# Causal row maxima of an attention block: the diagonal's 128 keys masked in SBUF instead of by products into PSUM

## The chip, the core and the metric

The kernel runs on one core of a Trainium2 chip. The metric is device time in microseconds (us). Three runs of the kernel before took 963.00, 969.34 and 960.15 us; their median is 963.0 us.

## What is computed

One transformer block over 8 sequences of 512 tokens with 256 channels: causal attention with 16 heads of 16 channels, plus a gated memory term, then a layer norm, then a mixture of 8 true experts, then a layer norm. Cut to what matters here:

```
scores = einsum('bhtd,bhsd->bhts', q, k) * scale        # per batch and head, 512 x 512
scores = where(causal, -inf, scores)
attn   = softmax(scores, axis=-1)                       # needs the maximum of each row t over s <= t
seq    = einsum('bhts,bhsd->bhtd', attn, v)
x      = layernorm(x + (seq + gated * mem_val) @ out_w.T + out_b)
expert = einsum('td,edh->teh', x, expert_w) + expert_b  # all 8 experts for every token
x      = layernorm(x + einsum('te,teh->th', combine_w, expert))
```

All data is float32.

## The kernel before

**Units and half steps.** Attention is worked off in 32 units, a unit being one batch b and a group g of four heads (`UNITS`, line 148). The main loop (lines 788 to 818) runs over units u, then over i = 0 to 3, then over pr = 0, 1. One pass of the innermost loop is called a half step here; there are eight to a unit. Two units are in work at once in each half step, in `products(u, i, pr)` (line 174):

- for unit m = u + 1, the products q k for the row maxima: `mx`, with 128 query tokens (block t) on the partitions and the n = 128, 512, 384 or 256 keys of the causal row (for i = 0, 1, 2, 3) along the free axis, for two heads (line 184). `mx` is a tile of two PSUM banks, one for each head, and there is one such tile (`psA`, bufs=1);
- for unit u (or u - 1 when i is 0), the products k q that become the softmax: `sc` (line 188), also one tile of two banks. ScalarE takes their exponential into `pe` (line 197), and GpSimd zeroes the masked part of its first 128 columns (line 199).

The two heads of `mx` and the two of `sc` use different groups of 32 rows of TensorE[...].

**The mask of the maxima.** After the products, line 191 adds a mask to the last 128 columns of each head's `mx`: a bfloat16 identity times a bfloat16 tile that holds -1e30 above the diagonal, accumulated in PSUM. Then VectorE takes the negated maximum over all n columns (line 194) into `negmax`, one column for each head and block. When all 16 columns of a unit are there, `turn_largest(u)` (line 203), called in half step (u, 0, 0), turns them by a TensorE transpose into `pt` (line 206), ScalarE copies the result (line 208), and a DMA on ScalarE's queue puts it as one more channel into the q tile of the unit (line 209), so that `sc` comes out with the maximum already taken off. The `sc` products of that unit begin in half step (u, 1, 0).

**Other fixed work of a half step.** In set half steps come `project_qk` (line 157, with two ScalarE evictions, line 161), `project_v` (line 167, one ScalarE copy, line 169), and, when pr is 1, `values` (line 220), the product of `pe` and v.

**The order of the work.** Instructions run on each engine in the order in which the Python code issues them (`in_this_order`, line 57). What fills a half step behind its fixed work is chosen by a planner at build time, `fill(need)` (line 755). It adds `need` (from `TAKE`, less `PQ`, `PV`, `PO`) and an allowance to a credit, capped at 3.0; the allowance is `EARLY` = 0.6 until the first batch's router is done (`ready`), and `MORE` = 0.9 from then on. It then lets chains of generators (`front`, `lines`, `memory_...`) and, while the credit is over 0.4, the bulk (`memory_sums`, `all_experts`) issue their next piece, and takes off what each `yield` says that it costs. `front(b)` (line 597) is the output projection, first norm and router of a batch, which must wait for that batch's attention (`done`). `all_experts(b)` (line 691) is its 16 expert pieces, of four matmul records each (line 707), each with two VectorE operations (line 711), and its second norm. `front` may be at most two batches ahead of the finished experts (line 624) and loads its input at most four ahead (line 552). After the attention, a loop (line 821) issues all that is left; it is called the tail here.

**Other engines' work that the steps touch.** GpSimd multiplies the attention output by the softmax denominators (`osb`, line 577) and prepares the residual (lines 560 to 566). VectorE evicts the output projection (lines 611 and 613) and the experts.

Of the kernel before, what the change touches and what calls it, by code (L numbers as in the profile page):

```python
# [9 lines left out]

F32 = mybir.dt.float32
BF16 = mybir.dt.bfloat16
AF = mybir.ActivationFunctionType
ALU = mybir.AluOpType
AX = mybir.AxisListType

P = 128
B, T, D, H, DH = 8, 512, 256, 16, 16
NT = T // P
KC = D // P  # L20
NG = 4
NE, NTRUE = 10, 8
MASKED = -1.0e30
# [1 line left out]


TAKE = (0.85, 1.6, 1.35, 1.1)
EARLY, MORE = 0.6, 0.9
PV, PQ, PO = 1.2, 2.15, (1.05, 0.85, 0.65, 0.45)
ROUNDS = (2, 1, 1, 1)  # L30
AHEAD = 5
# [36 lines left out]
def block_kernel(ctx, tc, x, xT, wqk, bqk, wtok, wod, memv, memvb, row, gw, we, eb, out):  # L68
    nc = tc.nc
    PS = bass.MemoryType.PSUM  # L70
    const = ctx.enter_context(tc.tile_pool(name="const", bufs=1))
# [3 lines left out]
    att = ctx.enter_context(tc.tile_pool(name="att", bufs=2))  # L75
# [28 lines left out]

    ws = const.tile([P, KC, NTRUE, D], F32, name="ws")
    nc.sync.dma_start(ws[:, :, 0, :], memv.rearrange("(k p) c -> p k c", p=P))
    ebs = const.tile([NTRUE, D], F32, name="ebs")
    wo = const.tile([P, KC, D], F32, name="wo")
    nc.sync.dma_start(wo, wod.rearrange("(k p) o -> p k o", p=P))
    mb = const.tile([P, KC, 2], F32, name="mb")  # L110
# [3 lines left out]
    for b in range(1, B):  # L114
# [3 lines left out]

    ident = const.tile([P, P], F32, name="ident")
    make_identity(nc, ident)  # L120
    identb = const.tile([P, P], BF16, name="identb")
    nc.vector.tensor_copy(identb, ident)

    mask_ts = const.tile([P, P], BF16, name="mask_ts")
    nc.gpsimd.memset(mask_ts, 0.0)
    nc.gpsimd.affine_select(out=mask_ts, in_=mask_ts, compare_op=ALU.is_ge, fill=MASKED,
                            base=0, pattern=[[-1, P]], channel_multiplier=1)
    half = const.tile([P, NT], F32, name="half")
    nc.gpsimd.memset(half, -0.5)
    first = const.tile([P, NE], F32, name="first")  # L130
# [18 lines left out]
    qk = {}  # L149
# [24 lines left out]
    def products(u, i, pr):  # L174
        m, t = u + 1, (0, 3, 2, 1)[i]
        v, j = (u, i - 1) if i else (u - 1, NT - 1)
        n = T - j * P
        mx = m < len(UNITS) and psA.tile([P, 2, T], F32, tag="mx", name=f"mx{m}_{t}_{pr}")
        sc = 0 <= v < len(UNITS) and psA.tile([P, 2, T], F32, tag="sc", name=f"sc{v}_{j}_{1 - pr}")
        for h in range(2):  # L180
            if mx:

                r = slice(32 * (2 * pr + h), 32 * (2 * pr + h) + 32)
                nc.tensor.matmul(mx[:, h, :n], qk[m, 0][r, n - P : n], qk[m, 1][r, :n], start=True, stop=False)  # L184
            if sc:

                r = slice(32 * (2 - 2 * pr + h), 32 * (2 - 2 * pr + h) + 32)
                nc.tensor.matmul(sc[:, h, :n], qk[v, 1][r, j * P : (j + 1) * P], qk[v, 0][r, j * P :], start=True, stop=True)  # L188
        if mx:
            for h in range(2):  # L190
                nc.tensor.matmul(mx[:, h, n - P : n], identb, mask_ts, start=False, stop=True)  # L191
            if m not in negmax:
                negmax[m] = att.tile([P, 4, NT], F32, name=f"negmax{m}", tag="negmax")
            nc.vector.tensor_reduce(negmax[m][:, 2 * pr : 2 * pr + 2, t], mx[:, :, :n], AX.X, ALU.max, negate=True)  # L194
        if sc:
            pe = att.tile([P, 2, T], F32, tag="pe", name=f"pe{v}_{j}_{1 - pr}", bufs=4)
            nc.scalar.activation(pe[:, :, :n], sc[:, :, :n], AF.Exp, scale=DH**-0.5)  # L197

            nc.gpsimd.affine_select(out=pe[:, :, :P], in_=pe[:, :, :P], compare_op=ALU.is_ge, fill=0.0,  # L199
                                    base=0, pattern=[[0, 2], [1, P]], channel_multiplier=-1)  # L200
            pes[j, 1 - pr] = pe

    def turn_largest(u):

        pt = bank(f"pt{u}")
        nc.tensor.transpose(pt[:H, :P], negmax.pop(u).rearrange("p j i -> p (j i)"), ident)
        nt = att.tile([H, P], F32, name=f"nt{u}", tag="nt")
        nc.scalar.copy(nt, pt[:H, :P])
        nc.scalar.dma_start(qk[u, 0][0 if u % 2 else DH :: 32], nt)

    negmax = {}
    pes, pos = {}, {}

    def values(u, j):
# [39 lines left out]
    def fold_values():  # L254

        wd, mv = wo, ws[:, :, 0, :]
        for c in range(KC):
            pw = bank(f"pw{c}")
            for k in range(KC):
                nc.tensor.matmul(pw[:, :D], mv[:, k, c * P : (c + 1) * P], wd[:, k, :],  # L260
                                 start=(k == 0), stop=(k == KC - 1))
            nc.scalar.copy(wt[:, c, CM : CM + D], pw[:, :D])
            yield 0.9
        for n in range(2):
            mbb = ws[:, :, 1 + n, :P]
            nc.vector.tensor_copy(mbb, bc(mb[:, :, n], 2, P))
            pw = bank(f"pwb{n}")
            for k in range(KC):
                nc.tensor.matmul(pw[:, :D], mbb[:, k, :], wd[:, k, :], start=(k == 0), stop=(k == KC - 1))
            if n == 0:  # L270
                nc.scalar.copy(b2, pw[:, :D])
            else:
                nc.vector.tensor_tensor(ob2, pw[:, :D], vec("ob"), ALU.add)
            yield 0.9
        for k in range(KC):
            nc.sync.dma_start(ws[:, k], we[:, k * P : (k + 1) * P, :].rearrange("e p h -> p e h"))
        nc.sync.dma_start(ebs, eb)

    memp = ctx.enter_context(tc.tile_pool(name="mem", bufs=1))
    turned, lined, gates = set(), set(), set()  # L280
# [268 lines left out]
    ffp = []  # L549

    def prepare(b):
        yield lambda: lines_over and b < left[0] + 4
        if not ffp:
            ffp.append(ctx.enter_context(tc.tile_pool(name="ff", bufs=2)))
        ff = ffp[0]

        xb = st[b]["xb"] = ff.tile([P, NT, D], F32, tag="x1", name=f"x1_{b}", bufs=4)
        nc.sync.dma_start(xb, x[b].rearrange("(c p) d -> p c d", p=P))
        yield POOL
        nc.gpsimd.tensor_tensor(xb, xb, bc(ob2, 1, NT), ALU.add)  # L560
        yield lambda: b // HALF in gates
        for c in range(0, NT, 2):
            yield POOL
            gb2 = ff.tile([P, 2, D], F32, tag="recs", name=f"gb2_{b}_{c}")
            nc.gpsimd.tensor_tensor(gb2, bc(b2, 1, 2), bc(gated[:, c : c + 2, b], 2, D), ALU.mult)
            nc.gpsimd.tensor_tensor(xb[:, c : c + 2], xb[:, c : c + 2], gb2, ALU.add)
        yield lambda: b in done
        recs = []
        for k in range(KC):
            recs.append(ff.tile([P, T], F32, name=f"recs{b}_{k}", tag="recs"))  # L570
            nc.sync.dma_start(recs[k], bc(st[b]["dr"][k], 1, DH))
        yield STEP
        yield STEP
        yield POOL
        for k in range(KC):
            o = st[b]["osb"][:, k, :]
            nc.gpsimd.tensor_tensor(o, o, recs[k], ALU.mult)
        yield STEP
# [112 lines left out]
    def all_experts(b):  # L691

        yield lambda: b in ready
        ff = ffp[0]
        x1, x1T, cw = (st[b][n] for n in ("x1", "x1T", "cw"))
        pc = bank(f"pc{b}")
        for c in range(NT):
            nc.tensor.matmul(pc[:NTRUE, c * P : (c + 1) * P], cw[:, c, :], ident, start=True, stop=True)
        cT = ff.tile([NTRUE, T], F32, tag="cT", name=f"cT_{b}", bufs=1)
        nc.scalar.copy(cT, pc[:NTRUE, :])  # L700
        yield 0.8
        mv2 = ff.tile([P, NT, 2], F32, tag="mv", name=f"mv2_{b}")
        for c in range(NT):
            for ep in range(NTRUE // 2):
                pe = bank(f"pex{b}_{c}_{ep}")
                for k in range(KC):
                    nc.tensor.matmul(pe, x1T[:, k, c * P : (c + 1) * P],  # L707
                                     ws[:, k, 2 * ep : 2 * ep + 2, :].rearrange("p e h -> p (e h)"),
                                     start=(k == 0), stop=(k == KC - 1))
                for e in range(2):  # L710
                    nc.vector.scalar_tensor_tensor(x1[:, c, :], pe[:, e * D : (e + 1) * D],  # L711
                                                   cw[:, c, 2 * ep + e : 2 * ep + e + 1], x1[:, c, :], ALU.mult, ALU.add)
                yield 1.75
            pb = bank(f"pbias{b}_{c}")
            nc.tensor.matmul(pb[:, :D], cT[:, c * P : (c + 1) * P], ebs, start=True, stop=True)  # L715
            nc.vector.tensor_tensor(x1[:, c, :], x1[:, c, :], pb[:, :D], ALU.add)
            stats(mv2, x1, c, f"b{b}")
            yield 0.45
        rr = root(mv2, f"b{b}")
        yield STEP  # L720
        for c in range(NT):
            norm(x1, x1, mv2, rr, c)
            nc.sync.dma_start(out[b, c * P : (c + 1) * P, :], x1[:, c, :])
        left[0] += 1
# [158 lines left out]
```

## Time and profile before

| | |
|---|---|
| median of three runs | 963.0 us |
| the profiled execution: its time, its span | 966.05 us, 964.2 us |
| TensorE (PE) busy, its weight loads | 885.6 us (92%), 426.0 us |
| VectorE (DVE) | 606.8 us (63%) |
| ScalarE (ACT) | 309.6 us (32%) |
| GpSimd (POOL) | 313.3 us (32%) |
| mean granted TensorE clock | 0.962 |

The span is the time from the first to the last instruction of the profiled execution; 1.85 us of its time lie around it. In the rows of operations, `L194 DVE ... x256 | 209.4, 818` means line 194, VectorE, 256 instructions, 209.4 us in total and 818 ns each in the mean. TensorE's records overlap and their ends are modelled, so the distance between the starts of two groups says more than their durations. A float32 matmul leaves two records.

### The profile page before, as it was taken

Reading aid. Unit: us, or ns where it says so; the run is one execution under the profiler, and the core shown is the slowest. Engines: PE = TensorE matmul, PEld = TensorE weight load, DVE = VectorE, ACT = ScalarE, POOL = GpSimd, SP = SyncE. Lnnn points to the kernel's source line nnn. Section 1 sums busy time; section 2 is a strip of 40 time slices with the busy share of each in tenths; the row PEclk is TensorE's granted clock in tenths of the full one; section 3 lists DMA queues with packets and bytes.
Section 4 is the critical chain, followed back from the end, with each engine's and each line's share of the span. In section 5 each row is a group of like instructions: output and inputs, shape, how many; then the busy total and the mean of one; then the engine's idle time right before and its main releaser. Section 6 shows DMA issues by size and latency. Waiting matters only on the chain.

```text
span 964.2 us, 14019 instructions
## 1 busy us (share of the span) xinstructions
PE 885.6 (92%) x5360; PEld 426.0 (44%) x5360; DVE 606.8 (63%) x1293; ACT 309.6 (32%) x606; POOL 313.3 (32%) x501
## 2 busy tenths in 40 slices
PE   6999987888788899999999999999999999979996
PEld 3544443444354454354544344543444344334442
DVE  1234657886966656756766866556655676577765
ACT  4164633344324233333323333332333332200000
POOL 1067763536363422521153113211231124230000
PEclk9799988999889799999999999999999999999998
DMA  7300000000000000100100000000000010020000
GB/s 247 95 11 16 11 7 4 3 2 24 4 23 24 13 14 10 39 2 3 39 30 1 2 26 23 23 1 22 28 23 1 4 46 23 3 67 1 22 22 22
DMA packets 25459, 23.67 MB, mean 25 GB/s; under 512 B 8324, under 2 KB 21132, under 8 KB 25392
## 3 DMA queue, kind: packets, MB, share of 16 engines
q1 hardware_dynamic: 24288, 22.22, 7.2%
q8 instruction: 42, 0.69, 0.3%
q10 hardware_dynamic: 1056, 0.40, 0.2%
q0 software_dynamic: 48, 0.16, 0.1%
q14 instruction: 25, 0.20, 0.1%
HBM read 16.73 MB, written 4.73 MB: 22 GB/s over the span
## 4 chain that ended last, share of the span: by engine, by line
PE 69%; DVE 16%; POOL 6%; DMA 3%; issue 3%; ACT 2%; SPq 0%; POOLq 0%; DVEq 0%; ACTq 0%
PE pex L707 22%; PE mx L184 14%; PE po L220 5%; PE pq L157 5%; DVE negmax L194 5%; PE mx L191 4%; PE pa L606 3%; PE pa L609 3%; PE pv L167 2%; PE sc L188 2%; DVE x L711 2%; DMA s<-w 2%; PE pbias L715 2%; PE pm L475 1%; DVE pr L485 1%
## 5 line engine op out<-in xcount | busy, mean ns | idle before, releaser
L197 ACT ACTIVATE pe<-sc 128x1024 f32<-128x1024 f32 (+3 forms) x256 | 180.1, 704 | 415.6 <-PE sc L188 400.0
L194 DVE TENSOR_REDUCE negmax<-mx 128x2 f32<-128x256 f32 (+3 forms) x256 | 209.4, 818 | 154.3 <-PE mx L191 153.9
L184 PE MATMUL mx<-qk,qk 32*128 32x128 f32 (+3 forms) x1024 | 226.7, 500 | 48.3 <-DVE negmax L194 45.8
L199 POOL TENSOR_SCALAR_AFFINE_SELECT pe<-pe 128x256 f32<-128x256 f32 x256 | 104.6, 409 | 475.4 <-ACT pe L197 475.0
L707 PE MATMUL pex<-ws,x1T 128*128 128x512 f32 x512 | 242.1, 606 | 3.7 <-DVE dn L683 2.1
L188 PE MATMUL sc<-qk,qk 32*128 32x512 f32 (+3 forms) x1024 | 217.4, 497 | 2.4 <-ACT pe L197 1.2
L711 DVE SCALAR_TENSOR_TENSOR x<-pex,cw,x 128x256 f32<-128x256 f32 x256 | 123.5, 482 | 92.8 <-PE pex L707 86.8
L184 PEld LDWEIGHTS mx<-qk,qk 32*128 32x128 f32 x1024 | 86.5, 190 | 170.6 <-DVE negmax L194 93.1
L707 PEld LDWEIGHTS pex<-ws,x1T 128*128 128x128 f32 x512 | 90.7, 190 | 112.2 <-issue 104.2
L220 PE MATMUL po<-pe,v_aug 128*32 128x512 f32 (+3 forms) x1024 | 98.9, 459 | 0.0
L188 PEld LDWEIGHTS sc<-qk,qk 32*128 32x128 f32 x1024 | 81.8, 189 | 11.5 <-ACT pe L197 4.7
L191 PEld LDWEIGHTS <-identb 128*128 128x128 bf16 x512 | 29.3, 98 | 119.3 <-issue 112.1
L191 PE MATMUL mx<-mask_ts,identb 128*128 128x128 bf16 x512 | 74.9, 229 | 0.0
L157 PE MATMUL pq<-xt,wq 128*128 128x512 f32 x128 | 65.5, 638 | 5.9 <-DMA xt<-in_xT 5.9
L161 ACT ACTIVATE qk<-pq,bq 128x512 f32<-128x512 f32 x64 | 46.3, 773 | 31.6 <-PE pq L157 31.6
L475 PE MATMUL pm<-ou,dm 128*128 128x144 f32 x256 | 48.4, 320 | 1.6 <-DVE pr L485 1.6
L475 PEld LDWEIGHTS pm<-ou,dm 128*128 128x128 f32 x256 | 39.2, 208 | 17.3 <-issue 12.4
L446 POOL TENSOR_TENSOR ou<-jw,jf 128x288 f32<-128x288 f32 x64 | 43.7, 688 | 1.3
L167 PE MATMUL pv<-wt,xt 128*128 128x256 f32 x128 | 37.9, 423 | 0.0
L585 POOL TENSOR_TENSOR rr_b<-rs_b,half 128x4 f32<-128x4 f32 x8 | 8.1, 1006 | 90.3 <-DVE rs_b L583 90.3
L483 DVE SCALAR_TENSOR_TENSOR ou<-pm,last,ou 32x288 f32<-32x288 f32 x48 | 25.2, 525 | 18.8 <-POOL ou L446 12.8
L319 PE MATMUL pl<-wt,xt 128*128 128x272 f32 x128 | 36.6, 423 | 0.0
(162 smaller groups left out, 872.9 us busy)
## 6 DMA issues: line engine op xcount, KB each, us to landing
xt<-in_xT SPq DMA_DIRECT2D x8, 512.0 KB
x<-in_x SPq DMA_DIRECT2D x8, 512.0 KB
recs<-dr SPq DMA_DIRECT2D x16, 256.0 KB
out_y<-x SPq DMA_DIRECT2D x32, 128.0 KB
ws<-in_we SPq DMA_DIRECT2D x2, 1024.0 KB
s<-w SPq DMA_DIRECT2D x8, 127.0 KB
qk<-nt ACTq DMA_DIRECT2D x32, 8.0 KB
wq<-in_wqk SPq DMA_DIRECT2D x3, 128.0 KB
```

The source lines that it names most:

```text
L157: nc.tensor.matmul(pq, wq[:, k, w, g // 2, :], xt[:, b, k, :], start=(k == 0), stop=(k == KC - 1))
L167: nc.tensor.matmul(pv[:, :D], xt[:, b, k, c * P : (c + 1) * P], wt[:, k, CV : CV + D], start=(k == 0), stop=(k == KC - 1))
L184: nc.tensor.matmul(mx[:, h, :n], qk[m, 0][r, n - P : n], qk[m, 1][r, :n], start=True, stop=False)
L188: nc.tensor.matmul(sc[:, h, :n], qk[v, 1][r, j * P : (j + 1) * P], qk[v, 0][r, j * P :], start=True, stop=True)
L191: nc.tensor.matmul(mx[:, h, n - P : n], identb, mask_ts, start=False, stop=True)
L194: nc.vector.tensor_reduce(negmax[m][:, 2 * pr : 2 * pr + 2, t], mx[:, :, :n], AX.X, ALU.max, negate=True)
L197: nc.scalar.activation(pe[:, :, :n], sc[:, :, :n], AF.Exp, scale=DH**-0.5)
L199: nc.gpsimd.affine_select(out=pe[:, :, :P], in_=pe[:, :, :P], compare_op=ALU.is_ge, fill=0.0, base=0, pattern=[[0, 2], [1, P]], channel_mu ...
L220: nc.tensor.matmul(pos[u][32 * h : 32 * h + 32, j * P :], v_aug[b % 2][:, j, 4 * (g // 2) + h, g % 2 : g % 2 + 2].rearrange("p q d -> p (q ...
L475: nc.tensor.matmul(pm[:, i * HALF * 36 : (i + 1) * HALF * 36], dms[h + i], ou[:, i], start=True, stop=True)
L707: nc.tensor.matmul(pe, x1T[:, k, c * P : (c + 1) * P], ws[:, k, 2 * ep : 2 * ep + 2, :].rearrange("p e h -> p (e h)"), start=(k == 0), sto ...
L711: nc.vector.scalar_tensor_tensor(x1[:, c, :], pe[:, e * D : (e + 1) * D], cw[:, c, 2 * ep + e : 2 * ep + e + 1], x1[:, c, :], ALU.mult, AL ...
```

## The change

The two mask products of each half step go, with the bfloat16 constants that fed them. In their place ScalarE copies the last n - 128 to n columns of `mx` (for two heads, 128x256 elements) into an SBUF tile `dia` (two buffers); GpSimd puts the causal mask in there; VectorE takes the maximum of the other n - 128 columns from PSUM at once (not for t = 0, which has none) and the maximum of `dia` in the next half step, after that half step's own reduction. The two results lie in two tiles, and `turn_largest` joins them with an elementwise minimum (they are negated) ahead of the transpose. The planner's allowance `MORE` goes from 0.9 to 1.3. The expert biases `ebs` move from the constant pool to the expert pool, their load to the first `prepare`, and the tile `nt` has one buffer instead of two.

```diff
-EARLY, MORE = 0.6, 0.9
+EARLY, MORE = 0.6, 1.3
...
-    identb = const.tile([P, P], BF16, name="identb")
-    nc.vector.tensor_copy(identb, ident)
-
-    mask_ts = const.tile([P, P], BF16, name="mask_ts")
-    nc.gpsimd.memset(mask_ts, 0.0)
-    nc.gpsimd.affine_select(out=mask_ts, in_=mask_ts, compare_op=ALU.is_ge, fill=MASKED,
-                            base=0, pattern=[[-1, P]], channel_multiplier=1)
...
-                nc.tensor.matmul(mx[:, h, :n], qk[m, 0][r, n - P : n], qk[m, 1][r, :n], start=True, stop=False)
+                nc.tensor.matmul(mx[:, h, :n], qk[m, 0][r, n - P : n], qk[m, 1][r, :n], start=True, stop=True)
...
+        behind = list(diagonal)
+        diagonal.clear()
         if mx:
-            for h in range(2):
-                nc.tensor.matmul(mx[:, h, n - P : n], identb, mask_ts, start=False, stop=True)
             if m not in negmax:
-                negmax[m] = att.tile([P, 4, NT], F32, name=f"negmax{m}", tag="negmax")
-            nc.vector.tensor_reduce(negmax[m][:, 2 * pr : 2 * pr + 2, t], mx[:, :, :n], AX.X, ALU.max, negate=True)
+                negmax[m] = [att.tile([P, 4, NT], F32, name=f"{n_}{m}", tag=n_) for n_ in ("negmax", "negdia")]
+
+            dia = att.tile([P, 2, P], F32, tag="dia", name=f"dia{m}_{t}_{pr}")
+            nc.scalar.copy(dia, mx[:, :, n - P : n])
+            nc.gpsimd.affine_select(out=dia, in_=dia, compare_op=ALU.is_ge, fill=MASKED,
+                                    base=0, pattern=[[0, 2], [-1, P]], channel_multiplier=1)
+            if t:
+                nc.vector.tensor_reduce(negmax[m][0][:, 2 * pr : 2 * pr + 2, t], mx[:, :, : n - P], AX.X, ALU.max, negate=True)
+            diagonal.append((negmax[m][1][:, 2 * pr : 2 * pr + 2, t], dia))
+        for to, dia in behind:
+            nc.vector.tensor_reduce(to, dia, AX.X, ALU.max, negate=True)
         if sc:
...
     def turn_largest(u):
         pt = bank(f"pt{u}")
-        nc.tensor.transpose(pt[:H, :P], negmax.pop(u).rearrange("p j i -> p (j i)"), ident)
-        nt = att.tile([H, P], F32, name=f"nt{u}", tag="nt")
+        most, least = negmax.pop(u)
+        nc.vector.tensor_tensor(least[:, :, 1:], least[:, :, 1:], most[:, :, 1:], ALU.min)
+        nc.tensor.transpose(pt[:H, :P], least.rearrange("p j i -> p (j i)"), ident)
+        nt = att.tile([H, P], F32, name=f"nt{u}", tag="nt", bufs=1)
...
-        nc.sync.dma_start(ebs, eb)
...
+            ffp.append(ffp[0].tile([NTRUE, D], F32, name="ebs", bufs=1))
+            nc.sync.dma_start(ffp[1], eb)
```

More of the change, by code (lines that the diff above doesn't have):

```diff
@@ L11 @@
 F32 = mybir.dt.float32
-BF16 = mybir.dt.bfloat16
 AF = mybir.ActivationFunctionType
@@ L106, in block_kernel @@
     nc.sync.dma_start(ws[:, :, 0, :], memv.rearrange("(k p) c -> p k c", p=P))
-    ebs = const.tile([NTRUE, D], F32, name="ebs")
     wo = const.tile([P, KC, D], F32, name="wo")
@@ L205, in turn_largest @@
         pt = bank(f"pt{u}")
-        nc.tensor.transpose(pt[:H, :P], negmax.pop(u).rearrange("p j i -> p (j i)"), ident)
-        nt = att.tile([H, P], F32, name=f"nt{u}", tag="nt")
+        most, least = negmax.pop(u)
+        nc.vector.tensor_tensor(least[:, :, 1:], least[:, :, 1:], most[:, :, 1:], ALU.min)
+        nc.tensor.transpose(pt[:H, :P], least.rearrange("p j i -> p (j i)"), ident)
+        nt = att.tile([H, P], F32, name=f"nt{u}", tag="nt", bufs=1)
         nc.scalar.copy(nt, pt[:H, :P])
         nc.scalar.dma_start(qk[u, 0][0 if u % 2 else DH :: 32], nt)
-    negmax = {}
+    negmax, diagonal = {}, []
     pes, pos = {}, {}
@@ L714, in all_experts @@
             pb = bank(f"pbias{b}_{c}")
-            nc.tensor.matmul(pb[:, :D], cT[:, c * P : (c + 1) * P], ebs, start=True, stop=True)
+            nc.tensor.matmul(pb[:, :D], cT[:, c * P : (c + 1) * P], ffp[1], start=True, stop=True)
             nc.vector.tensor_tensor(x1[:, c, :], x1[:, c, :], pb[:, :D], ALU.add)
```

## The prediction

> **What bounds the kernel now.** I read the chain that ended last first, then busy time in three stretches: before the first batch's router is done (311), to the end of attention (845), and the tail.
>
> ```profile
> PE 69%; DVE 16%; POOL 6%; DMA 3%; issue 3%; ACT 2%; SPq 0%; POOLq 0%; DVEq 0%; ACTq 0%
> ...
> 0.00:311.00 311.00, 264.51 (x1753) 138.99 (x1753) 182.34 (x332) 130.61 (x304) 149.33 (x252) 0.92 0.12 36
> 311.00:845.00 534.00, 516.36 (x3311) 237.39 (x3311) 342.89 (x748) 174.81 (x294) 150.50 (x239) 0.98 0.06 18
> 845.00:964.20 119.20, 104.72 (x304) 49.65 (x302) 81.57 (x214) 4.17 (x9) 13.46 (x11) 0.98 0.07 24
> ```
>
> After the stretch come its length, then PE, PEld, DVE, ACT and POOL busy. From 311 to 845 TensorE is busy 97% (17.6 us idle) and sets the end; before 311 it idles 46 us, waiting on others; the tail has 14.5 us of idle. So time taken from TensorE's queue counts whole in the middle stretch, about half in the first, and a wait put into that queue counts likewise.
>
> **Removed: the mask products.** What they occupy is seen from starts: mask start to the start of what follows.
>
> ```profile
> 500.86 0.69 PE L184 MATMUL mx<-qk,qk 32*128 32x512 f32 x1
> ...
> 501.93 0.29 PE L191 MATMUL mx<-mask_ts,identb 128*128 128x128 bf16 x2
> ...
> 502.14 0.43 PE L220 MATMUL po<-pe,v_aug 128*32 128x128 f32 x8
> ...
> 822.21 1.13 PE L188 MATMUL sc<-qk,qk 32*128 32x512 f32 x4
> ...
> 823.26 0.43 PE L220 MATMUL po<-pe,v_aug 128*32 128x128 f32 x8
> ```
>
> The products start the mask 1.07 us after themselves, the mask takes 0.21 more; in the last unit, which has no `mx` and no mask, the next work starts after 1.05. So the whole 0.21 goes. Over all half steps it is 0.22 us ahead of `values` (122 of them), 0.125 ahead of most else: 122 x 0.22 + 130 x 0.125 = 43 us. Some 172 half steps lie behind 311 (29 us, whole), 84 before (14 us, half): **-36 us**.
>
> **Added, in parallel.** ScalarE: 256 copies of 128x256 from PSUM; the `v_aug` copy of that shape takes 0.372 us, so +95 us (310 to 405 of 964). GpSimd: 256 selects of 128x256 at 0.409 (L199): +105 us (313 to 418). VectorE: the L194 forms take 1.224, 0.953, 0.679 and 0.417 us, so cutting 256 elements off and reducing them apart costs 0.953 + 0.417 - 1.224 = 0.146, three times of four: +28 us, and 32 minima. None becomes the bound by sum; in the first stretch, where VectorE's work already holds TensorE up, 64 half steps x 0.15 x half = **+5 us**. The ScalarE copy stands ahead of the exponential, which frees `sc`: 0.37 us later, hidden under `values` and the fill (1 to 3 us) that TensorE runs before the next `sc`; `PE sc L188 <- ACT pe L197` is 1.2 us in all. The select of `dia` stands ahead of that of `pe`: 0.41 later, and `values` reads it a half step on. VectorE reads `dia` a half step (3.1 us) after the copy, behind which at most one GpSimd operation of up to 2.4 us stands: hidden; without that cover the evictions of the fill, queued behind it, would be late. The `ebs` move is one 8 KB load, long before its use: nothing. One `nt` buffer: its reader, a DMA, is done a unit (24 us) before: nothing.
>
> **The new order on one bank.** `mx` is freed by VectorE's reduction alone:
>
> ```profile
> L194 DVE TENSOR_REDUCE negmax<-mx 128x2 f32<-128x1024 f32 x64 | 78.3, 1224 | 65.8 <-PE mx L191 65.7
> ...
> L169 ACT COPY v_aug<-pv 128x256 f32<-128x256 f32 x32 | 11.9, 372 | 19.8 <-PE pv L167 18.9 <-PE sc L188 0.6
> ...
> PE mx L184 <- DVE negmax L194: 45.8, 52, 4.2
> ```
>
> By the rows, copy and shortened reduction read different columns and could run together: mx free 0.95 us after the products, 0.4 to 0.5 earlier than by mask and reduction (0.2 + 1.22). The Trainium skill, "PSUM — Partial Sum Buffer", section "PSUM bank collisions raise a hardware error", speaks against that: two engines on one bank and quadrant collide even as two readers at different columns, so they must be ordered. Both instructions touch both banks, so I expect the reduction to wait for the copy: 0.37 + 0.95 + some 0.1 of handing over = 1.42, as before. No run here shows two engines at one bank. By the rows alone some 52 x 0.4 = 20 us of TensorE's 45.8 us of waits would go (sum 957); by the rule nothing. I take the rule: **0**, ends -20 and, where ScalarE is late with evictions of q, k (1.45 us a pair), +25.
>
> **The new wait: the transpose.** Before, `pt` used maxima finished a half step earlier. Now in (u, 0, 0) VectorE must finish the fill of the last half step, reduce the last `dia`, take the minimum; then TensorE transposes, and all of its queue stands behind that. At unit 21:
>
> ```profile
> 564.55 1.98 PE L707 MATMUL pex<-ws,x1T 128*128 128x512 f32 x4
> ...
> 566.58 1.00 DVE L711 SCALAR_TENSOR_TENSOR x<-pex,cw,x 128x256 f32<-128x256 f32 x2 [1.96 <-PE pex L707]
> ...
> 567.03 0.27 PE L206 MATMUL pt<-ident,negmax 128*16 128x128 f32 x1
> ```
>
> VectorE evicts the expert piece until 567.58; then 0.42 (reduction of 256) + 0.2 (small tensor_tensor, L658) + 0.1 = 568.3, while TensorE, without mask, is at `pt` at 566.9: a stall of 1.4 us. The DMA behind `pt` (2.4 us to its use, unit 19) moves with it, as does the work between: nothing more. Behind an output projection VectorE is 1.2 us behind `pt`, and it is 2.0; behind an empty half step 0.15. Worked out so at all 32 transposes of this trace, 34 us. The minimum also reads two SBUF operands: a 40-element operation of that kind (L680, usually 0.2) took 2.22 us beside a GpSimd operation of 2.36:
>
> ```profile
> 853.73 2.36 POOL L560 TENSOR_TENSOR x<-x,ob 128x1024 f32<-128x1024 f32 x1 [11.47 <-DMA x<-in_x]
> ...
> 853.92 2.22 DVE L680 TENSOR_TENSOR w<-w,ex 128x40 f32<-128x40 f32 x1
> ```
>
> The Trainium skill, "SBUF — State Buffer", "Who interferes with whom", gives this as a rule (such an operation and a GpSimd one that reads SBUF exclude each other); by the usual row the minimum costs 0.2, by the rule up to 0.4 more behind a select, 32 x 0.4 = 13 us as an upper end. With `MORE` 1.3 the half step before a transpose holds a piece in 20 of the last 21 units (next part): 20 x 1.35 = 27, and 8 for the earlier ones, where TensorE waits anyway: **+35 us**, ends 12 and 48.
>
> **MORE.** A batch (4 units, 32 half steps) earns: TAKE 4 x 2 x 4.9 = 39.2, less 1.2 (i = 0), 4 x 2.15 (PQ), 4 x 1.2 (PV), 4 x 3.0 (PO), plus 32 x 0.9: 41.4. It asks for 10.8 (front: 4 x 1.9 + 2 x 0.7 + 2 x 0.9) and 30.6 (experts: 0.8 + 16 x 1.75 + 4 x 0.45): 41.4 as well, so the experts stay some three batches behind. At 1.3 it earns 54.2. I followed `fill`'s bookkeeping through the yields for both values; for 0.9 it gives the trace's order (first expert batch done in unit 17, 465 us; second in 21, 571). At 0.9, 82 of 128 pieces are out by the end of attention, at 1.3 112: batches 0 to 6, with batch 7 alone left. A piece costs 1.77 us in the tail; in attention, half steps alike but for it differ by 1.2 (515.64 to 518.00 without, 562.91 to 566.47 with) to 1.8, by least squares over all 1.5; I take 1.6. So attention grows by 30 x 1.6 + 7 (biases, routers) = 55. The tail can't shrink below batch 7's own path from the last `values` (844.8), by the timeline's pieces: denominators out, inverted and back 10; GpSimd's products 3.7; projections and statistics 7.6 (865.7 to 873.3); norm 3; transposes and router products 3.5; expert choice 5.5; experts 4 x 7.69 (909.31 to 917.00 is one of four); end 8.4 (955.8 to 964.2): 73 us. Nothing is left to cover its first 33, where the profile before still had experts of batches 5 and 6. So the tail loses 119 - 74 = 45: **+10 us**, ends -5 (if that path is shorter) and +20 (a piece at 1.9).
>
> **Sum.** 966 - 36 + 5 + 0 + 35 + 10 = 980 us for an execution like the profiled one; the median of the runs lies 3 lower: **977 us**, own range 963 to 992. Chance 0.5.
>
> **Rivals.** (1) *Faster.* The stall at the transpose replaces waits that came later anyway: VectorE catches up while TensorE stands, and the waits on `negmax` (45.8 us) shrink by as much. Then 980 - 35 = 945, about 942 after the 3 us. For it: VectorE is 63% busy; against: from 311 on those waits are only 14.2 us. It decides once less than 0.5 us of each stall is net. Chance 0.18. (2) *ScalarE becomes a link in every half step*: the copy waits behind late evictions, the reduction behind the copy, the next `mx` behind both: 0.1 us x 256 = +25: 1002. For it: 1.45 us evictions in 64 half steps; against: ScalarE is 42% busy after. Chance 0.17. (3) *Even*: stalls of half size, tail covered: 963. Chance 0.15.
>
> **Ranges and chances.** 1% is 9.6 us, about what a measurement of this kernel tells from no change. The range holds forecast and rivals but half of (1) and a third of (2): 946 to 1004. Faster (below 953): 0.15, from (1). Within 1%: 0.15 from (3), 0.07 from the forecast's low end, a little of (1): 0.23. Slower: 0.62.
>
> **What would show it.** Right: `pt` preceded by TensorE idle that ends with VectorE's minimum, about 1.3 us, in some 25 units; next work 0.1 to 0.2 sooner behind the products; VectorE's `mx` reduction never starting before the copy's end; 112 pieces before attention ends, attention later, a tail of some 75 us with TensorE idle in its first half. Wrong: no idle ahead of `pt`; reduction beside copy; a tail over 90 us.

## The result and the profile after

The kernel after took 1023.1 us (median of 4 runs, 1020.76 to 1024.62), the kernel before beside it 964.13 us: a ratio of 1.061, 95% interval [1.055, 1.066]. The forecast was 977 us, its range 946 to 1004: the change costs 59 us, where 14 had been expected. (Against the kernel before that was run beside most of the experiments, 964.86 us, it is 58; that is used from there on.)

The profiled execution of the kernel after took 1024.62 us, with a span of 1022.9. Below it is cut at the transpose of unit 11, at the last `values` product, and at the end. Columns: length, then busy PE, PEld, DVE, ACT, POOL, then granted TensorE clock, DMA share, GB/s.

```profile
0.00:334.70 334.70, 259.39 (x1583) 133.46 (x1583) 198.76 (x431) 158.58 (x404) 190.34 (x350) 0.88 0.11 34
334.70:944.10 609.40, 563.02 (x3119) 250.43 (x3119) 390.03 (x981) 222.18 (x453) 217.45 (x401) 0.96 0.05 18
944.10:1022.90 78.80, 51.42 (x147) 27.86 (x146) 37.48 (x105) 2.57 (x5) 5.56 (x5) 0.78 0.07 21
```

The kernel before, cut at the same places, has 316.0, 528.3 and 119.9 us, at clocks of 0.91, 0.99 and 0.98. The stretches change by +19, +81 and -41 us. In the middle one TensorE, which was busy 97% of it, is busy 92% and works at a lower clock: it is at half speed for 43 us, against 12 before.

The waits of the kernel after (for whom, in total, times, longest):

```profile
DVE negmax L191 <- ACT dia L187: 126.9, 99, 6.4
PE mx L175 <- DVE negmax L191: 51.1, 48, 4.5
PE pt L208 <- DVE negdia L207: 48.7, 30, 3.7
```

The third line is the new wait: TensorE stands ahead of `pt` 30 times, 1.6 us each, for the minimum (line 207). The second is the old wait for the maxima, 45.8 us before: it didn't shrink. One of the 30, in the timeline of unit 23 (start, length, instruction; in brackets the idle time before it and who ended it):

```profile
676.50 0.37 ACT L187 COPY dia<-mx 128x256 f32<-128x256 f32 x1 [3.40 <-PE sc L179]
...
676.90 0.42 DVE L191 TENSOR_REDUCE negmax<-mx 128x2 f32<-128x256 f32 x1
...
677.16 1.98 PE L710 MATMUL pex<-ws,x1T 128*128 128x512 f32 x4
...
679.18 1.00 DVE L714 SCALAR_TENSOR_TENSOR x<-pex,cw,x 128x256 f32<-128x256 f32 x2 [1.53 <-PE pex L710]
...
680.10 0.41 DVE L194 TENSOR_REDUCE negdia<-dia 128x2 f32<-128x256 f32 x1
...
680.51 0.41 POOL L199 TENSOR_SCALAR_AFFINE_SELECT pe<-pe 128x256 f32<-128x256 f32 x1
...
680.55 0.40 DVE L207 TENSOR_TENSOR negdia<-negdia,negmax 128x12 f32<-128x12 f32 x1
...
681.00 0.28 PE L208 MATMUL pt<-ident,negdia 128*16 128x128 f32 x1 [1.42 <-DVE negdia L207]
```

Read from the third row on, this is the chain that the prediction drew for unit 21, at its predicted price of 1.4 us: expert piece, its evictions, the reduction of the last `dia`, the minimum, the transpose. The minimum takes 0.40 us beside a GpSimd select that starts just ahead of it. The first two rows show the order on the bank: VectorE's reduction begins as ScalarE's copy ends.

### The profile page after: what moved, and what is told of

Its sections match the earlier page's. It is cut to its first block, busy times and chain, and to the rows that moved or that the text cites. A ratio compares the mean times of both kernels' runs of the same rounds, so it can differ in the third digit from the quotient of the medians.

```text
span 1022.9 us, 14127 instructions
## 1 busy us (share of the span) xinstructions
PE 873.8 (85%) x4848; PEld 411.8 (40%) x4848; DVE 626.3 (61%) x1516; ACT 383.3 (37%) x862; POOL 413.3 (40%) x755
## 4 chain that ended last, share of the span: by engine, by line
PE 65%; DVE 18%; POOL 5%; ACT 4%; issue 4%; DMA 3%; SPq 0%; POOLq 0%; ACTq 0%; DVEq 0%
PE pex L710 22%; PE mx L175 13%; PE po L222 5%; PE pq L148 5%; DVE negmax L191 4%; PE pv L158 3%; PE pa L609 3%; PE pa L612 3%; PE pm L476 2%; DVE negdia L194 2%; PE sc L179 2%; DVE x L714 2%; ACT dia L187 1%; DVE ou L484 1%; PE pbias L718 1%
## 5 line engine op out<-in xcount | busy, mean ns | idle before, releaser
L188 POOL TENSOR_SCALAR_AFFINE_SELECT dia<-dia 128x256 f32<-128x256 f32 x256 | 105.2, 411 | 433.8 <-ACT dia L187 433.4
L710 PE MATMUL pex<-ws,x1T 128*128 128x512 f32 x512 | 252.3, 625 | 0.0
L187 ACT COPY dia<-mx 128x256 f32<-128x256 f32 x256 | 95.6, 373 | 393.0 <-PE sc L179 383.3
L179 PE MATMUL sc<-qk,qk 32*128 32x512 f32 (+3 forms) x1024 | 221.7, 505 | 5.3 <-DMA qk<-nt 5.3
L191 DVE TENSOR_REDUCE negmax<-mx 128x2 f32<-128x768 f32 (+2 forms) x192 | 131.8, 686 | 128.4 <-ACT dia L187 126.9
L194 DVE TENSOR_REDUCE negdia<-dia 128x2 f32<-128x256 f32 x256 | 104.8, 411 | 16.4 <-POOL dia L188 16.2
L476 PE MATMUL pm<-ou,dm 128*128 128x144 f32 x256 | 51.8, 340 | 0.0
L208 PE MATMUL pt<-ident,negdia 128*16 128x128 f32 x32 | 9.4, 293 | 48.7 <-DVE negdia L207 48.7
L612 PE MATMUL pa<-wo,osb 128*128 128x256 f32 x128 | 35.7, 399 | 11.5 <-POOL osb L580 11.5
L222 PEld LDWEIGHTS po<-pe,v_aug 128*32 128x32 f32 x1024 | 20.6, 110 | 59.0 <-issue 44.4
```

The source lines that it names most:

```text
L187: nc.scalar.copy(dia, mx[:, :, n - P : n])
L191: nc.vector.tensor_reduce(negmax[m][0][:, 2 * pr : 2 * pr + 2, t], mx[:, :, : n - P], AX.X, ALU.max, negate=True)
L194: nc.vector.tensor_reduce(to, dia, AX.X, ALU.max, negate=True)
L222: nc.tensor.matmul(pos[u][32 * h : 32 * h + 32, j * P :], v_aug[b % 2][:, j, 4 * (g // 2) + h, g % 2 : g % 2 + 2].rearrange("p q d -> p (q ...
L476: nc.tensor.matmul(pm[:, i * HALF * 36 : (i + 1) * HALF * 36], dms[h + i], ou[:, i], start=True, stop=True)
L710: nc.tensor.matmul(pe, x1T[:, k, c * P : (c + 1) * P], ws[:, k, 2 * ep : 2 * ep + 2, :].rearrange("p e h -> p (e h)"), start=(k == 0), sto ...
```

## The experiments

All times are medians, with the ratio to the kernel before run beside them on the same chip. The last four columns are of the profiled execution, whose time lies up to 5 us off the median (e2 above it, e6, e9 and e11 below).

| kernel | us | ratio [95%] | to unit 11's `pt` | to last `values` | tail | clock |
|---|---|---|---|---|---|---|
| before | 964 to 965 | 1 | 316 | 528 | 120 | 0.962 |
| after | 1023.1 | 1.061 [1.055, 1.066] | 335 | 609 | 79 | 0.921 |
| e1: before, MORE 1.3 | 987.9 | 1.025 [1.020, 1.029] | 315 | 596 | 78 | 0.942 |
| e5: e3, products put back | 1010.2 | 1.048 [1.043, 1.053] | 329 | 601 | 79 | 0.938 |
| e3: after, no join | 978.7 | 1.015 [1.012, 1.019] | 321 | 578 | 79 | 0.929 |
| e2: after, MORE 0.9 | 993.5 | 1.030 [1.026, 1.034] | 334 | 540 | 123 | 0.936 |
| e4: after, join early | 996.7 | 1.033 [1.027, 1.038] | 329 | 585 | 79 | 0.923 |
| e6: after, transpose later | 988.5 | 1.023 [1.018, 1.029] | 326 | 577 | 79 | 0.934 |
| e7: after, products in one half step of eight | 990.6 | 1.026 [1.019, 1.033] | 324 | 584 | 80 | 0.934 |
| e8: e4, MORE 0.9 | 965.0 | 1.002 [0.999, 1.004] | 324 | 514 | 122 | 0.951 |
| e9: e6, MORE 0.9 | 979.1 | 1.016 [1.011, 1.020] | 326 | 523 | 124 | 0.946 |
| e10: e9, first 12 units by products | 968.7 | 1.005 [1.003, 1.008] | 316 | 523 | 123 | 0.962 |
| e11: e3, MORE 0.9 | 958.7 | 0.995 [0.992, 0.997] | 320 | 510 | 121 | 0.944 |
| e12: e8, first 12 units by products | 959.3 | 0.995 [0.993, 0.997] | 321 | 518 | 120 | 0.951 |

The theory after the result was that the stall is as predicted and costs whole, and that the rest of the loss is MORE and clock. The rivals: that VectorE's or ScalarE's added work is what costs, that the removed products were worth less than thought, and that the clock falls because the products are gone and not because of the stalls.

**e1_more_alone**: the planner's constant by itself.

```diff
 (kernel before)
-EARLY, MORE = 0.6, 0.9
+EARLY, MORE = 0.6, 1.3
```

> The kernel before with only the planner's allowance raised from 0.9 to 1.3. Theory W (the wait of TensorE for VectorE ahead of the transpose, with the lower clock that it brings, is most of the loss, the moved work a small part): 970 to 985 us, tail some 75 us, no idle ahead of the transposes. Rival M (moving expert work out of the tail and leaving batch 7's path bare is most of the loss): 1000 us or more.

It took 987.9 us, 23 more than before and over the range. The middle stretch grows by 67 us and the tail shrinks by 42. Thirty pieces move out of the tail (112 of 128 are out at the last `values`, before 82), as predicted. They fill no gaps: TensorE's idle time in the middle is 17.5 us, before 16.5. And the tail that is left isn't run at full clock. The middle stretch and the tail of its trace, with the columns of the table of stretches above:

```profile
314.50:910.00 595.50, 578.01 (x3439) 263.43 (x3437) 377.32 (x842) 177.01 (x295) 155.79 (x242) 0.98 0.06 18
910.00:988.00 78.00, 51.01 (x147) 27.26 (x146) 37.48 (x105) 2.57 (x5) 5.55 (x5) 0.76 0.07 21
```

**e2_more_back**: the rest of the change by itself.

```diff
 (kernel after)
-EARLY, MORE = 0.6, 1.3
+EARLY, MORE = 0.6, 0.9
```

> The changed kernel with the allowance back at 0.9. Theory W: 1000 to 1015 us, since the stalls at the transposes stay, if somewhat shorter where the half step ahead of them is empty. Rival M: 960 to 980. Rival S (ScalarE's copy as a link in every half step is most of the loss): 1005 to 1020 too; the profile tells, by waits on the mx reduction instead of the transpose.

993.5 us, a little under the range: the rest costs 29 us by itself, and MORE 30 on top of it, where alone it cost 23. Taken singly the two make 52 of the 58 us.

**e3_no_join**: the wait taken away by taking its cause away. It leaves the last 128 keys out of each maximum (zero stands in for the first block, which has no others); all copies, selects and reductions stay, and the 32 minima go.

```diff
 (kernel after)
-        nc.vector.tensor_tensor(least[:, :, 1:], least[:, :, 1:], most[:, :, 1:], ALU.min)
-        nc.tensor.transpose(pt[:H, :P], least.rearrange("p j i -> p (j i)"), ident)
+        nc.tensor.transpose(pt[:H, :P], most.rearrange("p j i -> p (j i)"), ident)
```

> The changed kernel, but the transpose takes the maxima over the keys ahead of the last 128 (zero for the first block) and there is no minimum; copy, mask and reduction of the last 128 stay, their result is not used. This leaves out the last 128 keys of each row maximum. Theory W: the 48.7 us of waits ahead of the transposes go and the clock comes back to about 0.95 or better: 940 to 960 us. Rival M: 995 or more. Rival S: 1000 or more. Rival C (the granted clock falls because the mask products are gone, not because of the stalls): the clock stays near 0.92 and the time at 975 to 990.

978.7 us, over the range, since I had expected MORE to cost less; but 44.4 us under the kernel after. The 48.7 us of waits at `pt` are gone, and nearly all of it is gained: TensorE idles 40 us less. The waits for the maxima stay at 51.3 us:

```profile
PE mx L175 <- DVE negmax L192: 51.3, 46, 3.8
```

So the stall replaced no other wait. But the clock did not come back: over its four runs it is 0.929 to 0.934, in the kernel after 0.920 to 0.929, in e1 0.942 to 0.949. Time and clock are the numbers of rival C. Its cause is at most a part of it: MORE alone brings the clock from 0.962 to e1's, and with the products put back (e5, the next run) it is 0.930 to 0.941.

**e5_mask_back** takes e3 and puts a 128x128 product (of the identity with itself) back for each head's `mx`, so that e5 less e3 is the price of the products and e5 less e1 that of the added copies, selects and reductions.

```diff
 (e3_no_join)
-                nc.tensor.matmul(mx[:, h, :n], qk[m, 0][r, n - P : n], qk[m, 1][r, :n], start=True, stop=True)
+                nc.tensor.matmul(mx[:, h, :n], qk[m, 0][r, n - P : n], qk[m, 1][r, :n], start=True, stop=False)
...
+            for h in range(2):
+                nc.tensor.matmul(mx[:, h, n - P : n], identb, identb, start=False, stop=True)
```

> The kernel after without the join (the transpose takes the maxima ahead of the last 128 keys, as in the run without a join, 978.7 us), and with a product of 128x128 added into each mx tile's last 128 keys again, here of the identity with itself, so the numbers are not the reference's; everything that the SBUF path added stays. It prices the removed products alone. Theory: they are worth about 0.15 us of TensorE in each of 256 half tiles, some 20 to 40 us by my prediction's 36, less what the granted clock gives back: 995 to 1015. Rival, from the comparison of half steps (0.21 us in the half steps that go ahead of values, 0.07 in the others, 256 half steps): 36 x 0.5 = about 18, 990 to 1000. If the missing products only turn into other waits or a lower clock: 975 to 985.

1010.2 us. The products are worth 31.5 us, in the range. Between the profiles of e5 and e3 the half steps that go ahead of `values` lose a median of 0.21 to 0.22 us, the others 0.08. The added work costs 22.4 us, and that was the surprise: the prediction had 5. By the spans, 14 us of it lie ahead of unit 11's transpose, 5 in the middle. The first stretch of e1, then of e5:

```profile
0.00:314.50 314.50, 267.56 (x1777) 139.11 (x1778) 186.95 (x347) 131.34 (x306) 151.59 (x254) 0.91 0.12 36
0.00:328.50 328.50, 270.58 (x1778) 139.75 (x1779) 193.94 (x417) 156.75 (x402) 188.59 (x360) 0.90 0.11 35
```

TensorE idles 11 us more there. Waits behind that, over the whole span, the first line of e1, the others of e5:

```profile
PE mx L184 <- DVE negmax L194: 46.5, 45, 4.2
...
PE mx L177 <- DVE negmax L196: 49.5, 44, 3.6
...
PE sc L181 <- DMA qk<-nt: 3.9, 3, 1.8
```

In the first stretch alone the waits of `mx` for VectorE's maxima grow by 3.4 us. All of the 3.9 us of waits for `nt` (in e1 1.1 us) lie there, and a further 3.6 us in which `mx` waits for ScalarE's copy itself, in half steps with no reduction from PSUM (t = 0). TensorE is also at half clock for 8 us more of that stretch.

**e4_join_early** and **e6_turn_later** keep the numbers and mend the order. e4 reduces both diagonals of a unit's last half step at once and takes the minimum there, ahead of the fill:

```diff
 (kernel after)
+        if mx and i == NT - 1 and pr == 1:
+            behind += diagonal
+            diagonal.clear()
         for to, dia in behind:
             nc.vector.tensor_reduce(to, dia, AX.X, ALU.max, negate=True)
+        if mx and i == NT - 1 and pr == 1:
+            most, least = negmax[m]
+            nc.vector.tensor_tensor(least[:, :, 1:], least[:, :, 1:], most[:, :, 1:], ALU.min)
...
-        nc.vector.tensor_tensor(least[:, :, 1:], least[:, :, 1:], most[:, :, 1:], ALU.min)
```

> The changed kernel, but in the last half step of a unit VectorE reduces the last two diagonals and takes the minimum at once, ahead of that half step's fill, instead of behind it in the next; all is computed. VectorE then waits some 0.6 us for GpSimd there, under TensorE's values and fill. Theory W: within 10 us of the run without the join, 945 to 970 us, no more than 10 us of idle ahead of the transposes. If VectorE's wait for GpSimd costs as much as the stall: 1000 or more.

e6 leaves the minimum where it is (`join_largest` is that line alone) and issues the transpose behind the fill of half step (u, 0, 0):

```diff
 (kernel after)
                     if i == 0 and 0 <= u < U:
-                        turn_largest(u)
+                        join_largest(u)
...
                 fill(need)
+                if pr == 0 and i == 0 and 0 <= u < U:
+                    turn_largest(u)
```

> The kernel after with the minimum where it is and the transpose issued after the fill of the half step (u,0,0), not ahead of it: the same work in another order. If the 48.7 us at the transpose are a stall that only the order makes, it goes and the time is near that of the run without a join, 978.7 us, plus 32 transposes of 0.3 us: 978 to 990. If the negated maxima then reach the q rows too late and TensorE waits at sc instead: 995 to 1020, with a wait of sc on the DMA of nt.

e4 took 996.7 us, 26 less than the kernel after but well over its range; e6 988.5, 35 less and in its range. What is left of the wait, in e4 and in e6:

```profile
PE pt L213 <- DVE negdia L200: 7.5, 11, 1.3
```

```profile
PE pt L211 <- DVE negdia L205: 10.8, 13, 2.6
```

In e4 all but 7.5 of 48.7 us of the wait are gone, but the time is 18 us above that of the kernel without a join. Of those, 16 are in the two attention stretches, where it is at half clock for 14 us more; the minima and the reductions that are now in front of the evictions may make up the rest, which no run takes apart.

**e7_hybrid** gives the last half step of each unit its mask by products, as before, and takes the minima there.

```diff
 (kernel after)
+            if last:
+                for h in range(2):
+                    nc.tensor.matmul(mx[:, h, n - P : n], identb, mask_ts, start=False, stop=True)
+                nc.vector.tensor_reduce(negmax[m][1][:, 2 * pr : 2 * pr + 2, t], mx[:, :, :n], AX.X, ALU.max, negate=True)
```

(To make room for the constants, the tiles `nt` and `rec` share one buffer in e7, e10 and e12, and `rec` has one instead of two in e5.)

> The kernel after, but the last half step of each unit gets its mask by mask products, as before, and its maxima are joined at once; the other seven of eight half steps go by way of SBUF. No late reduction stands ahead of the transpose. If lateness at the transpose is what costs, the wait there falls from 48.7 to below 8 us and the time to 978 to 988 (978.7 without a join, plus some 4 us of products and minima). If any join costs as much as the early one did (996.7): 990 to 1000.

990.6 us: the number of the other case, that any join costs as much. The wait at `pt` is down to 1.6 us, yet 12 us against e3 remain. The products of one half step in eight would be 4 of these, an eighth of 31.5 (an estimate). Against e3, then, a join costs 18 us in e4, 10 in e6 and 12 in e7, with 7.5, 10.8 and 1.6 us of visible wait at `pt`: in e6 the wait can be all of it, in e4 and e7 it isn't, and what the rest is stays open.

**e8_early_less**, **e9_later_less**, **e11_no_join_less**: e4, e6 and e3 with MORE 0.9.

```diff
 (e4_join_early, e6_turn_later, e3_no_join)
-EARLY, MORE = 0.6, 1.3
+EARLY, MORE = 0.6, 0.9
```

> The kernel after with both diagonals of a unit's last half step reduced and joined ahead of the fill (996.7 us with MORE 1.3), and MORE 0.9. If the planner's constant costs here what it cost alone (988.0 against 964.9, 23 us) and from the kernel after (30 us): 967 to 975, slower than before by under 1%. If the two don't add, since the earlier join already leaves TensorE the room that MORE took: 980 to 997.

> The transpose after the fill of the half step (u,0,0), as in the run of 988.5 us, and MORE 0.9. MORE has been worth 23 us on the kernel before, 30 on the kernel after and 32 with the early join. If it is worth as much here: 957 to 966, a ratio of 0.992 to 1.001 to the kernel before. If the later transpose lived from the pieces that MORE moved: 968 to 980.

> The run without a join (978.7 us; it leaves the last 128 keys out of each maximum) with MORE 0.9: the floor of this change, products gone and nothing late ahead of the transpose. If MORE is worth its 23 to 32 us here too: 947 to 956. If without a wait at the transpose the moved pieces cost less: 958 to 970.

e8 took 965.0 us, even with the kernel before and better than expected; e11 958.7, a little over its range and in that of its rival (moved pieces cost less where nothing waits at the transpose); e9 979.1, the rival's number. MORE has cost 23 us in the kernel before, 30 in the kernel after, 32 in e4, 20 in e3 and only 9 in e6. The last is explained in part: with MORE 0.9 some fills between the minimum and the transpose are empty, and in three of the last 21 units of e9 TensorE waits there 1.3 to 1.8 us, which at MORE 1.3 happened in none. The wait at `pt` is 16.6 us in e9, 10.8 in e6. So the later transpose did live from the pieces that MORE moved; some 6 us of that are seen, the rest of the 11 to 22 by which MORE gave less here is open.

**e10_first_masked** and **e12_first_masked_early**: the mask by products for units 0 to 11, by way of SBUF from unit 12 on, with the order of e9 and of e8.

```diff
 (e9_later_less, e8_early_less)
+        direct = m < 12
...
+            if direct:
+                for h in range(2):
+                    nc.tensor.matmul(mx[:, h, n - P : n], identb, mask_ts, start=False, stop=True)
+                nc.vector.tensor_reduce(negmax[m][1][:, 2 * pr : 2 * pr + 2, t], mx[:, :, :n], AX.X, ALU.max, negate=True)
+            else:
```

> As the run before it in this list (transpose after the fill, MORE 0.9), but the first 12 of 32 units get their mask by mask products and are transposed where the kernel before does it; units 12 to 31 go by way of SBUF. Theory: the added copies, selects and reductions cost 19 us with the products put back, 14 of them ahead of unit 11's transpose, where VectorE and the maxima set the pace and not TensorE; so the first stretch comes back to the 316 us of the kernel before and the time falls by a further 5 to 12 us: 947 to 960. Rival: the products cost in the first stretch as much as the SBUF path does, and nothing is gained: 960 to 970.

> The first 12 units by mask products, units 12 to 31 by way of SBUF with both diagonals of a unit's last half step reduced and joined ahead of the fill, the transpose where the kernel before has it, MORE 0.9. If stretches can be put together: 316 us up to unit 11's transpose (kernel before, and the run with the first units masked), 514 up to the last values product and 122 of tail (the early join with MORE 0.9) make a span of 952 and a time of 952 to 959, a ratio of 0.987 to 0.995. Rival: the granted clock gives the difference back, 959 to 966.

e10 took 968.7 us, in the rival's range because e9, from which it was counted, had come out higher; it gains 10.4 us on e9 (it also has the first 12 transposes back in their old place), which is the gain that the theory had. e12 gains 5.7 on e8. Both say that ahead of unit 12, where TensorE waits for the maxima, the SBUF path costs more than the products that it saves. How much more, the profiles tell less well: the first stretch of e10 is back at 316 us, but that of e12, which issues the same work in the same order up to there, took 321, with 56 us at half clock against 42. e12 took 959.3 us, where its two expectations meet: 0.5% under the kernel before, with an interval that leaves 1 out, even with the kernel without a join (e11), and the best of those here that take the maximum over all keys. It has what the change can give here: products out of the stretch that TensorE bounds, the path left out of the stretch that it doesn't, the join early, the tail filled.

## Why the prediction was wrong

One path through the runs splits the 58 us: before, e1, e5, e3, after. The last two columns tell what each step adds to TensorE's idle time (of the profiled executions) and to its time at half clock (median over all runs of each kernel, worked out from span and mean clock: 73, 108, 127, 138 and 155 us).

| step of the prediction | predicted | measured | from | idle | half clock |
|---|---|---|---|---|---|
| MORE | +10 | +23 | e1 less before | +13 | +35 |
| added work: VectorE +5, bank order 0 | +5 | +22 | e5 less e1 | +14 | +19 |
| mask products | -36 | -31.5 | e3 less e5 | +4 | +11 |
| stall at the transpose | +35 | +44 | after less e3 | +40 | +17 |
| sum | +14 | +58 | | +71 | +82 |

Another path gives other shares: with MORE 0.9 the stall costs 35 us (e2 less e11), and MORE without a join 20 (e3 less e11).

**The mechanism was right.** TensorE does stand ahead of `pt` until VectorE's minimum, in 30 units of 32, the minimum is slowed by GpSimd (0.17 us in nine units with no GpSimd instruction beside it, 0.35 in the mean of all 32), and e3 shows that this is the largest loss. The 30.4 us from unit 11 on were put at 27. What was mis-sized is "8 for the earlier ones, where TensorE waits anyway": units 0 to 10 have 18.3 us. A wait that ends in the same engine's next result isn't covered by the waits around it; those for the maxima grew, in the first stretch, from 32.8 to 36.8 us.

**The step that failed is the price of the added work**: 5 us for VectorE, and 0 for the new order on the bank, whose upper end, "where ScalarE is late with evictions of q, k (1.45 us a pair), +25", was left out of the sum. It measured 22. The order itself is as predicted: none of the 192 reductions starts before the copy's end, and 136 start within 0.1 us of it. The trace agrees with the Trainium skill, "PSUM — Partial Sum Buffer", "PSUM bank collisions raise a hardware error", as far as it goes: the two instructions never overlap. And as an average the 0 holds: from the start of the mask, which e1 and e5 both have, `mx` is free after 1.68 us in e1 and 1.69 in e5 (mean of the first stretch). But the average hides two kinds of half steps. With a reduction from PSUM (n = 256 to 512) the release comes some 0.1 to 0.24 us later in the median; without one (n = 128) 0.44 earlier. So early releases don't seem to pay TensorE back for the late ones: of the 11 us by which it idles longer in the first stretch, some 6 are waits for `mx`, and 3 are waits for `nt`, which stands in ScalarE's queue with the copies. In the middle, where most half steps have a fill behind their products, the added work cost 5 us. No run takes ScalarE's copies apart from VectorE's reductions, or the single `nt` buffer, which the prediction put at nothing, from that queue, so how the 22 us divide among them stays open.

Whatever lies in this row and whatever in that of the products, e3 less e1 has both: -9 us, where -31 had been predicted. There TensorE's idle time grows by 17 us, 14 of them in the first stretch, where 5 had been put down, and it is at half clock for 30 us more, where nothing had been. Rival (2) named 25 us for the added work, but that it comes near 22 is in part luck: it had them in every half step, and the waits for `mx` are a quarter of it. It had been held against the forecast as another case, while both happen together.

**MORE** lost twice. The 30 pieces moved as drawn, but one was put at 1.6 us: 67.2 us of growth, less the 7 predicted for biases and routers, over 30 pieces is 2.0, about the 1.98 us that its matmuls take. And the tail lost 42 us, not 45. The granted clock has a part in both: in e1 the middle is at half clock for 10 us more than before, the tail for 37 us instead of 5. The tail's length was otherwise as drawn, 79 us against 74, and TensorE idles in its first half as foretold, here 9.64 us for GpSimd's products (kernel after):

```profile
955.86 1.22 PE L612 MATMUL pa<-wo,osb 128*128 128x256 f32 x2 [9.64 <-POOL osb L580]
```

**The products** were nearly right. From their start to that of the next work, at full clock, e3 is 0.22 us shorter than e5 ahead of `values` and 0.125 ahead of most else, as predicted; over the whole half step 0.08 is left of the latter.

**The clock was in no term**, without a reason given. The kernel after runs at 0.921 in the mean, the one before at 0.962. TensorE's idle time grew from 78.6 to 149.1 us, its busy time fell by only 11.8, although the products were worth over 31: the difference, 20 us or more, is an estimate of what work done at half clock adds. These 20 us aren't one more row of the table; they are spread over its rows, and by the last column MORE brought the most. Whether the removal of the products brought any isn't certain: the runs of e5 have 119 to 142 us at half clock, those of e3 129 to 139.

Of the rivals, (1) falls with e3 and (3) with e1 and e3: neither was the stall of half size nor the tail covered.

## What to carry to other kernels

Before a mask, a bias or another few columns are moved from the busiest engine to two idle ones, ask what then stands between a result and the engine that waits for it: here the idle engines had time for the work, but the chain copy, select, reduction, join came to lie ahead of an instruction at the head of TensorE's in-order queue. Join as soon as the last part is there and before optional work is queued (e8 against e2: 28 us), and leave the old way in a stretch that the relieved engine doesn't bound (e10 against e9: 10 us, e12 against e8: 6). An average of 0 need not be a price of 0: early results may bring nothing where late ones cost. Cases that don't exclude each other belong into the sum with their chances, not beside it as rivals.

## What was not expected of the hardware

The trace of the kernel after has TensorE's clock in 38 stretches, at full and at half speed by turns, and all but the last are 3.41 us long or a whole multiple of that. It can fall after a gap of 2 us. Two windows of the kernel after, one with a stall at `pt` in it and the one right behind it, and the transpose from its timeline:

```profile
534.40:537.80 3.40, 1.28 (x11) 0.40 (x9) 3.23 (x10) 0.96 (x3) 0.77 (x2) 1.00 0.00 0
537.80:544.70 6.90, 6.90 (x24) 2.65 (x24) 4.48 (x8) 0.91 (x3) 0.71 (x2) 0.51 0.00 1
```

```profile
537.63 0.28 PE L208 MATMUL pt<-ident,negdia 128*16 128x128 f32 x1 [2.12 <-DVE negdia L207]
```

TensorE is busy 1.28 of 3.40 us, and then granted 0.51 for 6.9 us. At half clock an expert piece takes twice as long; from another such stretch, against the 1.98 us shown above:

```profile
399.23 3.76 PE L710 MATMUL pex<-ws,x1T 128*128 128x512 f32 x4
```

So this stall of 2.1 us cost some 3 more behind it, an estimate: 6.9 us at half speed do the work of 3.5. The Trainium skill, "TensorE: Matmul & The Clock Gate", Part 1, "What's actually happening", has the length (3413 ns, half clock after an idle window); it asks for a window that is idle, and here one with 1.28 us of work was followed by half clock. No threshold comes out of this trace. Of 165 windows of that length at full clock between 347 and 940 us, 23 are busy under 70%; half clock follows four of them, and it also follows one window that is busy 71% and one that is busy throughout.

The scatter of one and the same kernel is of this kind too. Over 97 runs of the kernel before, spans of 955 to 959 us go with a mean clock of 0.967 to 0.971, spans of 964 to 968 with 0.957 to 0.962; a line through all of them gives 0.4 us of span for each us at half clock. That is why a few tenths of a per cent need many runs here.
